# Layer 0's mixing: half of the evictions on ScalarE from 512-column blocks, a quarter of them summed by VectorE

## The chip, the cores and the metric

The kernel runs on one core of a Trainium2 chip. The metric is device time in microseconds (us), median of three runs; less is better. The core has TensorE (PE, matrix products into PSUM), VectorE (DVE), ScalarE (ACT), GpSimd (POOL) and SyncE (SP, here the queue of loads). Each engine works through its own queue in order and waits on semaphores. PSUM has 8 banks; the kernel takes them in four pairs, and calls a pair a bank, and so does this text.

## The reference, cut to what matters

Two graph layers on x of 8 batches, 2048 nodes and 64 channels. In layer 0 every node has its own weights, a mix of 16 shared ones by its embedding:

```python
w = jnp.einsum('nd,dkio->nkio', embedding, weight)      # D = 16, K = 3
b = jnp.einsum('nd,do->no', embedding, bias)
As = [jnp.eye(N), A, 2.0 * (A @ A) - jnp.eye(N)]
x_g = jnp.einsum('knm,bmc->bnkc', jnp.stack(As, 0), x)
out = jnp.einsum('bnki,nkio->bno', x_g, w) + b
x = layernorm(x + out)
```

Layer 1 applies adj twice more and shared weights, adds and normalises again.

## The kernel before

The nodes are 16 tiles of 128. The program has these stages: the first hop (adj times x), the second hop as seven products of half-size blocks, layer 0's mixing (226 to 526 us of the span), the third hop as seven products again, and the last hop with the output.

**Mixing.** For a tile t, `mix0` needs three operands: x, the first hop and the second hop, each transposed and in three parts for precision (`high`, `low`, `mixed`: lines 309 to 322, function `parts`). One product mixes them with the 16 shared weights d, and the 16 results are added up with the node's embedding as factor. Eight batches come as two groups g of four. The work is cut into eight pieces (g, i), each filling one bank `pm`:

- `by_batch` (i = 0 or 1): two batches, d = 0 to 7. 9 pairs of matmuls with 512 columns. ACT evicts it with eight instructions (line 423), each scaled by the embedding, into two SBUF tiles `aside`. When both pieces of a group are there, POOL sums them with three additions (`sum_aside`, line 440) and adds the result to the accumulator `acc` (`add_aside`, line 445).
- `by_four` (i = 4 or 5, and 2 or 3 in place of a `by_batch`): four batches, four d. 18 pairs of matmuls with 256 columns. DVE evicts it with four instructions that multiply by the embedding and add to `acc` (line 433); each of them waits for the one before.

A pair is two matmuls on the two halves of the 128 rows. Before, a tile has two pieces by batch and six by four; the last tile, t = 15, has four of each.

**What stands between the pieces.** The list `at[n]` says what is issued before piece n: the steps of the next tile's operands (`of_x`, `of_hop`, `of_second`), the steps of the previous tile's layernorm (`next(norm)`), `begin_sum` (which starts the next `acc` on POOL), `times_r` (a scaling on POOL for the tile after next), the transposes of the normalised tile (`hT`), and POOL's sums. At a tile's end `project` sends the previous tile's result through layer 1's weights, ACT copies it out (line 475), and the first two steps of x's parts for the tile after next follow. The order of the source is the order of each engine's queue here (`ordered`). In the last tile, `early` starts the operands of the third hop's first steps.

`parts` makes `mixed` in one of two ways: with `quick` by one DVE instruction (line 317), else by an ACT copy and a POOL addition (lines 319 and 320). Before, quick is used for tile 0 alone.

**Buffers.** `hl` tiles come from a pool of HL = 8, `raw` tiles (loads, `aside` and the second hop's parts) from one of RAW = 5. `seven_products` takes four banks for its first product's sums: `sums` is two pairs, and products alternate between them (line 656).

Of the kernel before, what the change touches and what calls it, by code (L numbers as in the profile page):

```python
# [18 lines left out]
P = 128  # L19
# [6 lines left out]
HL = 8  # L26
RAW = 5
# [12 lines left out]
def pattern(  # L40
# [106 lines left out]
    def node_bias(pb):  # L147

        eT, b0_sb = bias_sb[:, : N // 4], bias_sb[:, N // 4 :]
        for j in range(4):  # L150
            for g in range(4):
                q = slice(32 * g, 32 * g + D)
                nc.tensor.matmul(  # L153
                    pb[g // 2][:, g % 2, j * C : (j + 1) * C], lhsT=eT[q, j * P : (j + 1) * P], rhs=b0_sb[q],
                    start=True, stop=True, tile_position=(32 * g, 0),
                )
# [5 lines left out]
    wl = work2.tile([P, 5, C], F32, tag="t0", name="wl")  # L162
    bias_sb = work2.tile([P, N // 4 + C], F32, tag="t0", name="bias_sb")

    loads = [(bias_sb, bias), (pack_sb, pack[:, : NT * D]), (wl.rearrange("p k o -> p (k o)"), pack[:, NT * D + C :])]
# [193 lines left out]
    def layernorm(src):  # L359
# [10 lines left out]
        ordered(nc.vector.tensor_reduce(ss, sq, AX.X, ALU.add))  # L370
        sd, r0, va, q, r = [work.tile([P, B], F32, tag=f"{name}{B}", name=name) for name in ("ln_sd", "ln_r0", "ln_v", "ln_q", "ln_r")]
# [30 lines left out]
    def mix0(t, tt, acc, at, pieces):  # L402
# [14 lines left out]
        def by_batch(g, i):  # L417
            pm = bank("pm").rearrange("p j (d c) -> p j d c", c=C)
            block(pm, 2 * g + i, slice(0, 2 * DG))
            if i == 0:  # L420
                aside[g] = [rawp.tile([P, DG, 2, 2, C], F32, tag="raw", name="aside") for _ in range(2)]
            for d in range(2 * DG):
                ordered(nc.scalar.activation(aside[g][d // DG][:, d % DG, :, i, :], pm[:, :, d, :], AF.Copy, scale=e(d)))  # L423
# [22 lines left out]

        for n, (g, i) in enumerate([*pieces, (None, None)]):
            for work_here in at[n]:
                if isinstance(work_here, tuple):
                    for part in work_here[0]:  # L450
                        {"sum": sum_aside, "add": add_aside}[part](work_here[1])
# [134 lines left out]
    def seven_products(s, to, sums, more, wait=4, raw=()):  # L586
# [31 lines left out]
        def step(p, kk):  # L618
# [38 lines left out]
            def use(got):  # L657
                if p == 0 and kk == 0:
                    sums.extend([bank("accT") for _ in range(2)] for _ in range(2))
# [65 lines left out]
    def operands(t, quick=False):  # L725
# [5 lines left out]
        def begin(k, src):  # L731
# [6 lines left out]
        def of_x():  # L738
            yield from begin(0, xt)

        def of_hop(pt=None):
            yield from begin(1, transposed(z[1][t], pt))

        def of_second():
            yield from begin(2, by_pair(z[2][t]))
# [92 lines left out]
    }, wait=2)  # L838
# [18 lines left out]
    for t in range(NT):  # L857
        got, last = {}, t == NT - 1
        at = [[] for _ in range(9)]
        n1, n2, n3 = [lambda: next(norm)] * 3 if t else [nothing] * 3  # L860

        if not last:
# [3 lines left out]
            at[2] += [go(of_hop), n1, go(of_hop), go(of_hop), n2]  # L866
            if t + 2 < NT:
                at[2] += [lambda: times_r(t + 2)]
                at[4] += [lambda: got.update(coming=operands(t + 2))]
            at[3] += [n3, go(of_second), lambda: got.update(acc=begin_sum(t + 1))]  # L870
            at[4] += [go(of_second), go(of_second)]
            at[6] += [(("sum", "add"), 0)]
            at[7] += [lambda: got.update(hT=transpose(h, "hT"))] if t else []
            pieces = [(0, 0), (0, 4), (0, 5), (1, 2), (0, 1), (1, 3), (1, 4), (1, 5)]
        else:
            at[1] += [n1, n2]
# [5 lines left out]
            at[7] += [(("sum",), 1), lambda: early(2, "y_low"), lambda: early(3, "y_high")]  # L882
            at[8] += [(("add",), 1), lambda: early(3, "y_low")]
            pieces = [(0, 0), (0, 1), (0, 4), (1, 0), (0, 5), (1, 1), (1, 4), (1, 5)]
        norm_now = mix0(t, tt, acc, at, pieces)
# [10 lines left out]
    todo.extend([nothing] * 4 + [lambda: next(norm)] * 3)  # L896
# [479 lines left out]
```

## Time and profile before

| | us |
|---|---|
| median of 3 runs | 764.98 (764.36 to 765.15) |
| profiled execution | 764.04 |
| its span, first to last instruction | 762.3 |
| layer 0's mixing in it | 226.2 to 526.3 |
| a steady tile of the mixing | 18.96 |

In a line of the profile, "out<-in 128x256 x376 | 181.0, 482 | 44.0 <-PE pm L409 32.0" means 376 instructions, 181.0 us busy in union, 482 ns each on average, and 44.0 us in which the engine stood idle just before them, 32.0 of it until PE had finished `pm`. PEld is the weight load of PE. Matmuls overlap, so their length is not their cost; the distance between two starts is.

One tile in the middle, busy us by engine: PE 18.96, DVE 15.26, ACT 10.69, POOL 15.13, of 18.96.

### The profile page before, as it was taken

Reading aid. Unit: us, or ns where it says so; the run is one execution under the profiler, and the core shown is the slowest. Engines: PE = TensorE matmul, PEld = TensorE weight load, DVE = VectorE, ACT = ScalarE, POOL = GpSimd, SP = SyncE. Lnnn points to the kernel's source line nnn. Section 1 sums busy time; section 2 is a strip of 40 time slices with the busy share of each in tenths; the row PEclk is TensorE's granted clock in tenths of the full one; section 3 lists DMA queues with packets and bytes.
Section 4 is the critical chain, followed back from the end, with each engine's and each line's share of the span. In section 5 each row is a group of like instructions: output and inputs, shape, how many; then the busy total and the mean of one; then the engine's idle time right before and its main releaser. Section 6 shows DMA issues by size and latency. Waiting matters only on the chain.

```text
span 762.3 us, 16926 instructions
## 1 busy us (share of the span) xinstructions
PE 753.6 (99%) x6634; PEld 660.6 (87%) x6634; DVE 560.2 (73%) x1159; ACT 406.7 (53%) x896; POOL 269.7 (35%) x297
## 2 busy tenths in 40 slices
PE   9999999999999999999999999999999999999996
PEld 6888888888889999999999999998888888888885
DVE  6768867678757888888888888877688648668663
ACT  5456533877745555555555555558887663112111
POOL 0000000000026877777777777777100000011441
PEclk9999999999999999999999999999999999999999
DMA  8998996555520000000000000003454444565631
GB/s 325 346 393 282 350 312 233 154 177 162 171 69 17 20 20 15 20 18 16 16 16 17 15 16 3 2 16 87 135 167 151 130 154 142 175 177 175 208 127 46
DMA packets 73558, 96.69 MB, mean 127 GB/s; under 512 B 4864, under 2 KB 48384, under 8 KB 73344
## 3 DMA queue, kind: packets, MB, share of 16 engines
q1 hardware_dynamic: 62064, 76.66, 31.8%
q10 hardware_dynamic: 11408, 18.89, 6.6%
q8 instruction: 54, 0.88, 0.5%
q14 instruction: 32, 0.26, 0.1%
HBM read 76.65 MB, written 18.87 MB: 125 GB/s over the span
## 4 chain that ended last, share of the span: by engine, by line
PE 98%; DVE 1%; issue 0%; ACT 0%; DVEq 0%
PE pm L409 36%; PE accT L664 27%; PE acc L254 15%; PE a L254 10%; PE accT L254 6%; PE pu L466 2%; PE pt L300 1%; PE first L143 1%; PE accT L814 1%; DVE acc L433 1%; PE accT L466 0%; PE accT L153 0%; PE accT L300 0%; ACT sq L994 0%; DVE z L289 0%
## 5 line engine op out<-in xcount | busy, mean ns | idle before, releaser
L433 DVE SCALAR_TENSOR_TENSOR acc<-pm,pack_sb,acc 128x256 f32<-128x256 f32 x376 | 181.0, 482 | 44.0 <-PE pm L409 32.0
L409 PE MATMUL pm<-wh,hl 64*128 64x512 f32 (+1 forms) x1332 | 208.0, 303 | 0.0
L664 PE MATMUL accT<-s,hl 128*128 128x512 f32 x896 | 205.9, 390 | 0.8 <-DVE acc L433 0.8
L409 PE MATMUL pm<-wm,parts 64*128 64x512 f32 (+1 forms) x1332 | 203.5, 296 | 0.0
L409 PE MATMUL pm<-wl,parts 64*128 64x512 f32 (+1 forms) x1332 | 203.4, 296 | 0.0
L664 PEld LDWEIGHTS accT<-s,hl 128*128 128x128 f32 x896 | 167.5, 188 | 36.5 <-issue 1.6
L409 PEld LDWEIGHTS pm<-wh,hl 64*128 64x128 f32 x1332 | 130.9, 187 | 4.0 <-issue 0.4
L409 PEld LDWEIGHTS pm<-wl,parts 64*128 64x128 f32 x1332 | 130.8, 187 | 3.7
L409 PEld LDWEIGHTS pm<-wm,parts 64*128 64x128 f32 x1332 | 130.5, 187 | 3.8
L652 ACT CAST s<-raw 128x1024 fp32r<-128x1024 bf16 x104 | 109.9, 1057 | 37.9 <-ACT hl L234 23.4
L254 PE MATMUL acc<-hl,s 128*128 128x512 f32 x512 | 116.8, 390 | 0.0
L254 PEld LDWEIGHTS acc<-hl,s 128*128 128x128 f32 x512 | 96.2, 188 | 20.5 <-issue 0.3
L423 ACT ACTIVATE aside<-pm,pack_sb 128x128 f32<-128x128 f32 x272 | 74.0, 383 | 48.9 <-PE pm L409 48.1
L715 POOL TENSOR_TENSOR z<-z,rrow 128x512 f32<-128x512 f32 x16 | 21.1, 1320 | 212.4 <-DVE z L688 212.4
L234 ACT CAST hl<-z 128x256 fp32r<-128x256 f32 (+1 forms) x96 | 47.7, 515 | 60.1 <-PE acc L254 24.1
L440 POOL TENSOR_TENSOR aside<-aside 128x1024 f32<-128x1024 f32 (+2 forms) x51 | 75.3, 1476 | 4.2 <-ACT aside L423 1.6
L254 PE MATMUL a<-hl,s 128*128 128x512 f32 (+1 forms) x352 | 73.4, 370 | 0.0
L254 PEld LDWEIGHTS a<-hl,s 128*128 128x128 f32 x352 | 61.9, 188 | 11.3
L320 POOL TENSOR_TENSOR parts<-parts 128x512 fp32r<-128x512 f32 x45 | 58.2, 1294 | 35.1 <-DVE parts L314 27.5
L238 DVE TENSOR_TENSOR hl<-z,hl 128x512 fp32r<-128x512 f32 (+1 forms) x96 | 54.7, 577 | 12.9 <-ACT hl L234 10.1
L287 POOL TENSOR_TENSOR z<-z,got 128x512 f32<-128x512 f32 x3 | 4.8, 1631 | 144.4 <-ACT got L286 144.4
L254 PE MATMUL accT<-hl,s 128*128 128x512 f32 x192 | 44.3, 390 | 0.0
(136 smaller groups left out, 814.4 us busy)
## 6 DMA issues: line engine op xcount, KB each, us to landing
raw<-in_adj SPq DMA_DIRECT2D x58, 512.0 KB, 6.1
raw<-sums_of SPq DMA_DIRECT2D x64, 256.0 KB, 2.9
sums_of<-z ACTq DMA_DIRECT2D x16, 512.0 KB, 6.6
raw<-quarters SPq DMA_DIRECT2D x32, 256.0 KB, 2.7
raw<-in_adj SPq DMA_DIRECT2D x16, 384.0 KB, 3.5
quarters<-seen ACTq DMA_DIRECT2D x16, 256.0 KB, 5.8
xt<-in_xT SPq DMA_DIRECT2D x16, 256.0 KB, 2.7
z<-in_x SPq DMA_DIRECT2D x15, 256.0 KB, 6.8
```

Source lines behind the costliest of these rows:

```text
L234: ordered(nc.scalar.copy(to[0], src))
L238: ordered(nc.vector.tensor_tensor(to[1], src, to[0], ALU.subtract))
L254: nc.tensor.matmul(accs[i], lhsT=s[:, i * P : (i + 1) * P], rhs=hl[h], start=(first and h == 0), stop=(last and h == 1),)
L320: ordered(nc.gpsimd.tensor_tensor(mixed, mixed, low, ALU.add))
L409: nc.tensor.matmul(pm[:, j], lhsT=tt[k][n][q, lhsT, :], rhs=w_parts[n][k][q, ds, :], start=(k == 0 and n == 0), stop=(k == 2 and n == 2),)
L423: ordered(nc.scalar.activation(aside[g][d // DG][:, d % DG, :, i, :], pm[:, :, d, :], AF.Copy, scale=e(d)))
L433: ordered(nc.vector.scalar_tensor_tensor(part, got, e(dg * DG + d), part, ALU.mult, ALU.add))
L440: ordered(nc.gpsimd.tensor_tensor(to, to, more, ALU.add))
L466: nc.tensor.matmul(pm[:, j, i * 3 * C : (i + 1) * 3 * C], lhsT=hT[q, 2 * g + i, :], rhs=v[q], start=True, stop=True,)
L652: ordered(nc.scalar.copy(s, got["raw"]))
L664: nc.tensor.matmul(acc[i][:, c], lhsT=hl[h][:, i * P : (i + 1) * P], rhs=S[:, c * 512 : (c + 1) * 512], start=(kk == 0 and h == 0), stop=( ...
L715: ordered(nc.gpsimd.tensor_tensor(to, to, r, ALU.mult))
```

## The change

- In tiles 0 to 14 the pieces are now (1,0), (0,4), (1,1), (0,0), (0,1), (0,5), (1,4), (1,5): four by batch, four by four, and the last three on DVE.
- For group 1 the ACT evictions write into tiles laid out as [2, 64, 8]: d is innermost, so each instruction writes single elements 32 bytes apart, and DVE sums over d with one `tensor_reduce` per piece from contiguous memory (`reduce_aside`) and adds both results to `acc` (`add_reduced`). Group 0 goes by POOL as before.
- `mixed` of x and of the second hop is quick on DVE in all tiles; that of the first hop stays on ACT and POOL.
- Steps between pieces move: hop's transposes, `begin_sum` and `times_r` come before piece 1, the layernorm has one step more (`root` is ACT's square root, apart from the sum before it), and POOL's sum and add are two places.
- In the last tile the low half of the third early operand is issued after the last piece.
- HL is 7 and RAW is 6. The bias is loaded in two parts. The third hop pairs its four sum banks (0, 2) and (1, 3).

```diff
@@ -23,8 +23,8 @@
 DG = 4
 EPS = 1e-5
 FIRST = 8
-HL = 8
-RAW = 5
+HL = 7
+RAW = 6
 WARM = 12
 SLOTS = 3
 SPLIT = 4096.0
@@ -146,7 +146,7 @@
 
     def node_bias(pb):
 
-        eT, b0_sb = bias_sb[:, : N // 4], bias_sb[:, N // 4 :]
+        eT, b0_sb = bias_sb, wl[:, 5]
         for j in range(4):
             for g in range(4):
                 q = slice(32 * g, 32 * g + D)
@@ -159,10 +159,11 @@
         to = ebias[:, 8 * h : 8 * h + 8, :].rearrange("p (g t) c -> p g (t c)", g=2)
         ordered(nc.vector.tensor_copy(to, pb[h][:, :, : 4 * C]))
 
-    wl = work2.tile([P, 5, C], F32, tag="t0", name="wl")
-    bias_sb = work2.tile([P, N // 4 + C], F32, tag="t0", name="bias_sb")
-
-    loads = [(bias_sb, bias), (pack_sb, pack[:, : NT * D]), (wl.rearrange("p k o -> p (k o)"), pack[:, NT * D + C :])]
+    wl = work2.tile([P, 6, C], F32, tag="t0", name="wl")
+    bias_sb = work2.tile([P, N // 4], F32, tag="t0", name="bias_sb")
+
+    loads = [(bias_sb, bias[:, : N // 4]), (wl[:, 5], bias[:, N // 4 :]), (pack_sb, pack[:, : NT * D])]
+    loads += [(wl[:, :5].rearrange("p k o -> p (k o)"), pack[:, NT * D + C :])]
     loads += [(bias1, pack[:, NT * D : NT * D + C]), (rrow, diag.to_broadcast([P, N]))]
 
     def weights():
@@ -368,6 +369,7 @@
         yield
         ss = work.tile([P, B], F32, tag="ln_ss", name="ss")
         ordered(nc.vector.tensor_reduce(ss, sq, AX.X, ALU.add))
+        yield
         sd, r0, va, q, r = [work.tile([P, B], F32, tag=f"{name}{B}", name=name) for name in ("ln_sd", "ln_r0", "ln_v", "ln_q", "ln_r")]
         ordered(nc.scalar.activation(sd, ss, AF.Sqrt, bias=eps, scale=1.0 / C))
         yield
@@ -399,7 +401,7 @@
 
 
 
-    def mix0(t, tt, acc, at, pieces):
+    def mix0(t, tt, acc, at, pieces, on_vector=()):
 
         def block(pm, lhsT, ds):
             for k in range(3):
@@ -417,10 +419,15 @@
         def by_batch(g, i):
             pm = bank("pm").rearrange("p j (d c) -> p j d c", c=C)
             block(pm, 2 * g + i, slice(0, 2 * DG))
-            if i == 0:
-                aside[g] = [rawp.tile([P, DG, 2, 2, C], F32, tag="raw", name="aside") for _ in range(2)]
+            if g in on_vector:
+                aside[g, i] = rawp.tile([P, 2, C, 2 * DG], F32, tag="raw", name="aside")
+                to = [aside[g, i][:, :, :, d] for d in range(2 * DG)]
+            else:
+                if i == 0:
+                    aside[g] = [rawp.tile([P, DG, 2, 2, C], F32, tag="raw", name="aside") for _ in range(2)]
+                to = [aside[g][d // DG][:, d % DG, :, i, :] for d in range(2 * DG)]
             for d in range(2 * DG):
-                ordered(nc.scalar.activation(aside[g][d // DG][:, d % DG, :, i, :], pm[:, :, d, :], AF.Copy, scale=e(d)))
+                ordered(nc.scalar.activation(to[d], pm[:, :, d, :], AF.Copy, scale=e(d)))
 
         def by_four(g, dg):
             dg -= 2
@@ -444,11 +451,21 @@
             one = aside[g][0][:, 0].rearrange("p j i c -> p (j i) c")
             ordered(nc.gpsimd.tensor_tensor(part, part, one, ALU.add))
 
+        def reduce_aside(i):
+            if i == 0:
+                aside["sum"] = xcpool.tile([P, 2, 2, C], F32, tag="ln_xc", name="both")
+            ordered(nc.vector.tensor_reduce(aside["sum"][:, i], aside[1, i], AX.X, ALU.add))
+
+        def add_reduced(_):
+            part = acc[:, 4:8, :].rearrange("p (j i) c -> p i j c", j=2)
+            ordered(nc.vector.tensor_tensor(part, part, aside["sum"], ALU.add))
+
+        does = {"sum": sum_aside, "add": add_aside, "reduce": reduce_aside, "add_reduced": add_reduced}
         for n, (g, i) in enumerate([*pieces, (None, None)]):
             for work_here in at[n]:
                 if isinstance(work_here, tuple):
                     for part in work_here[0]:
-                        {"sum": sum_aside, "add": add_aside}[part](work_here[1])
+                        does[part](work_here[1])
                 else:
                     work_here()
             if n < len(pieces):
@@ -583,7 +600,7 @@
         (S4, "B22", (0, 1)), ((0, 1), "B21", (0, 0)), ((1, 1), "T4", (1, 0)),
     )
 
-    def seven_products(s, to, sums, more, wait=4, raw=()):
+    def seven_products(s, to, sums, more, wait=4, raw=(), pairs=((0, 1), (2, 3))):
 
 
 
@@ -656,7 +673,8 @@
 
             def use(got):
                 if p == 0 and kk == 0:
-                    sums.extend([bank("accT") for _ in range(2)] for _ in range(2))
+                    four = [bank("accT") for _ in range(4)]
+                    sums.extend([four[a], four[b]] for a, b in pairs)
                 acc, hl, S = sums[p % 2], got["hl"], got["s"]
                 for i in range(2):
                     for h in range(2):
@@ -728,7 +746,7 @@
         load(nc.sync, xt, xT[t])
         tt = [None] * 3
 
-        def begin(k, src):
+        def begin(k, src, quick):
             where, tag = ((rawp, "raw"), (spool, "s"))[k != 2]
             high = hpool.tile([P, B // 2, P], F32R, tag="hl", name="hl")
             pair = where.tile([P, 2, B // 2, P], F32R, tag=tag, name="parts")
@@ -736,13 +754,13 @@
             return parts(src, tt[k], by_half if k == 1 else lambda to: to, quick)
 
         def of_x():
-            yield from begin(0, xt)
+            yield from begin(0, xt, True)
 
         def of_hop(pt=None):
-            yield from begin(1, transposed(z[1][t], pt))
+            yield from begin(1, transposed(z[1][t], pt), quick)
 
         def of_second():
-            yield from begin(2, by_pair(z[2][t]))
+            yield from begin(2, by_pair(z[2][t]), True)
 
         return tt, of_x(), of_hop, of_second()
 
@@ -835,7 +853,7 @@
         (0, 6): [last_projected],
         **{(2 + t // KK, t % KK): [lambda t=t: add_bias(t)] for t in range(NT)},
         3: quarter_back(1, 1, 1), 4: quarter_back(0, 1, 0), 5: quarter_back(0, 0, 1),
-    }, wait=2)
+    }, wait=2, pairs=((0, 2), (1, 3)))
 
     third_got = {}
 
@@ -857,32 +875,37 @@
     for t in range(NT):
         got, last = {}, t == NT - 1
         at = [[] for _ in range(9)]
-        n1, n2, n3 = [lambda: next(norm)] * 3 if t else [nothing] * 3
+        n1, n2, root, n3 = [lambda: next(norm)] * 4 if t else [nothing] * 4
 
         if not last:
             following, of_x, of_hop, of_second = coming
             of_hop = of_hop()
             at[1] += [go(of_x)] * (1 if t else 3)
-            at[2] += [go(of_hop), n1, go(of_hop), go(of_hop), n2]
+            at[1] += [n1, lambda: got.update(acc=begin_sum(t + 1))]
             if t + 2 < NT:
-                at[2] += [lambda: times_r(t + 2)]
+                at[1] += [lambda: times_r(t + 2)]
+            at[1] += [go(of_hop)]
+            at[2] += [n2, go(of_hop), go(of_hop), (("reduce",), 0)]
+            at[3] += [root]
+            at[4] += [n3, go(of_second), (("reduce",), 1), (("add_reduced",), 1)]
+            if t + 2 < NT:
                 at[4] += [lambda: got.update(coming=operands(t + 2))]
-            at[3] += [n3, go(of_second), lambda: got.update(acc=begin_sum(t + 1))]
-            at[4] += [go(of_second), go(of_second)]
-            at[6] += [(("sum", "add"), 0)]
+            at[5] += [go(of_second), go(of_second)]
+            at[6] += [(("sum",), 0)]
             at[7] += [lambda: got.update(hT=transpose(h, "hT"))] if t else []
-            pieces = [(0, 0), (0, 4), (0, 5), (1, 2), (0, 1), (1, 3), (1, 4), (1, 5)]
+            at[7] += [(("add",), 0)]
+            pieces, on_vector = [(1, 0), (0, 4), (1, 1), (0, 0), (0, 1), (0, 5), (1, 4), (1, 5)], (1,)
         else:
-            at[1] += [n1, n2]
+            at[1] += [n1, n2, root]
             at[2] += [n3, lambda: early(0, "y_high", *s)]
             at[3] += [(("sum",), 0), lambda: early(0, "y_low")]
             at[4] += [lambda: early(1, "y_high", *s)]
             at[5] += [lambda: early(1, "y_low")]
             at[6] += [(("add",), 0), lambda: got.update(hT=transpose(h, "hT")), lambda: early(2, "y_high")]
-            at[7] += [(("sum",), 1), lambda: early(2, "y_low"), lambda: early(3, "y_high")]
-            at[8] += [(("add",), 1), lambda: early(3, "y_low")]
-            pieces = [(0, 0), (0, 1), (0, 4), (1, 0), (0, 5), (1, 1), (1, 4), (1, 5)]
-        norm_now = mix0(t, tt, acc, at, pieces)
+            at[7] += [(("sum",), 1), lambda: early(3, "y_high")]
+            at[8] += [(("add",), 1), lambda: early(2, "y_low"), lambda: early(3, "y_low")]
+            pieces, on_vector = [(0, 0), (0, 1), (0, 4), (1, 0), (0, 5), (1, 1), (1, 4), (1, 5)], ()
+        norm_now = mix0(t, tt, acc, at, pieces, on_vector)
         if t:
             project(t - 1, got["hT"])
         if "coming" in got:
@@ -893,7 +916,7 @@
         h = next(norm)
         if not last:
             tt, acc = following, got["acc"]
-    todo.extend([nothing] * 4 + [lambda: next(norm)] * 3)
+    todo.extend([nothing] * 4 + [lambda: next(norm), lambda: (next(norm), next(norm)), lambda: next(norm)])
 
 
     def count(name, src):
```

## The prediction

> **What bounds the kernel now.** I read the page first: its engine line, its slices, and the chain of waits by engine.
>
> ```profile
> PE 753.6 (99%) x6634; PEld 660.6 (87%) x6634; DVE 560.2 (73%) x1159; ACT 406.7 (53%) x896; POOL 269.7 (35%) x297
> PE   9999999999999999999999999999999999999996
> ...
> PE 98%; DVE 1%; issue 0%; ACT 0%; DVEq 0%
> PE pm L409 36%; PE accT L664 27%; PE acc L254 15%; PE a L254 10%; PE accT L254 6%; PE pu L466 2%; PE pt L300 1%; PE first L143 1%; PE accT L814 1%; DVE acc L433 1%; PE accT L466 0%; PE accT L153 0%; PE accT L300 0%; ACT sq L994 0%; DVE z L289 0%
> ```
>
> TensorE (PE) is busy in every slice and owns the chain, and the clock was granted at 0.999. "Busy" only means that a matmul is in flight, so next comes the view of waits on PE, which is short:
>
> ```profile
> PE first L143 <- DVE part L144: 1.3, 1, 1.3
> PE accT L664 <- DVE acc L433: 0.8, 1, 0.8
> ```
>
> Columns: total us, times, longest. In the 300 us of layer 0's mixing (L409) PE waits for nobody. So a faster VectorE or ScalarE saves nothing there; fewer or better filled matmuls save time, and so does the one 0.8 us wait. The price of a matmul is the distance between starts, which PE's timeline gives (start, length of the group, count):
>
> ```profile
> 302.39 0.40 PE L409 MATMUL pm<-wm,parts 64*128 64x512 f32 x2
> 302.62 0.29 PE L409 MATMUL pm<-wh,hl 64*128 64x256 f32 x2
> ...
> 304.76 0.41 PE L300 MATMUL pt<-ident,z 64*128 64x64 f32 x8
> ...
> 309.38 0.40 PE L409 MATMUL pm<-wh,hl 64*128 64x512 f32 x2
> ...
> 311.44 0.28 PE L409 MATMUL pm<-wh,hl 64*128 64x256 f32 x2
> ...
> 315.76 0.41 PE L300 MATMUL pt<-ident,xc 64*128 64x64 f32 x8
> ```
>
> A piece of 9 pairs of 512 columns lasts 309.38 to 311.44 = 2.06 us. Two pieces of 18 pairs of 256 last 311.44 to 315.76 = 4.32, so 2.16 each; the one at 302.62 took 2.14. The same columns cost 0.08 to 0.10 us more in blocks of 256: twice as many pairs, each with a small fixed cost. I take 0.09.
>
> The 0.8 us wait stands where layer 0 ends. PE and VectorE (DVE) there:
>
> ```profile
> 526.28 1.47 PE L466 MATMUL pu<-v,hT 64*128 64x192 f32 x16
> 527.69 1.20 PE L664 MATMUL accT<-s,hl 128*128 128x512 f32 x4
> 529.65 0.93 PE L664 MATMUL accT<-s,hl 128*128 128x512 f32 x3 [0.76 <-DVE acc L433]
> ...
> 526.30 1.24 DVE L238 TENSOR_TENSOR hl<-z,hl 128x256 fp32r<-128x256 f32 x1
> 527.47 2.03 DVE L433 SCALAR_TENSOR_TENSOR acc<-pm,pack_sb,acc 128x256 f32<-128x256 f32 x4
> ```
>
> The fifth matmul needs the bank that DVE's last four evictions free. They start at 527.47 because the low half of the third early operand, 1.24 us, stands before them, although their piece was done at 526.28.
>
> Last, a steady tile's busy time by engine, and the prices:
>
> ```profile
> 357.29:376.25 18.96, 18.96 (x289) 18.32 (x287) 15.26 (x32) 10.69 (x33) 15.13 (x18) 1.00 0.06 17
> ...
> L423 ACT ACTIVATE aside<-pm,pack_sb 128x128 f32<-128x128 f32 x272 | 74.0, 383 | 48.9 <-PE pm L409 48.1 <-POOL aside L440 0.8
> L319 ACT ACTIVATE parts<-hl 128x512 fp32r<-128x512 f32 x45 | 29.9, 664 | 0.5
> L314 DVE TENSOR_TENSOR parts<-z,hl 128x512 fp32r<-128x512 f32 x16 | 18.0, 1122 | 6.9 <-ACT hl L312 6.9
> L314 DVE TENSOR_TENSOR parts<-xt,hl 128x512 fp32r<-128x512 f32 x16 | 11.1, 692 | 17.3 <-ACT hl L312 17.3
> ```
>
> The first line is length, PE, PEld, DVE, ACT, POOL. All four others have room under 18.96.
>
> **What the Trainium skill says.** "Advanced Engine Details and Errata", Instruction Support, lists no faster mode for tensor_reduce, so about one element a cycle. The trace agrees: 680 ns for 512 elements (L362), 344 for 192, a slope of 1.05 ns. The same page, GPSIMD Details, says Pool shares an interface with DVE and conflicts with DVE instructions that have two SBUF inputs. The trace agrees: the L314 row from z takes 1.12 us while POOL works, the one from xt 0.69 while POOL mostly idles. "SBUF — State Buffer", Door 1, says each access that crosses to a new 16-byte line pays a penalty, without a size. ScalarE (ACT) will write single 4-byte elements 32 bytes apart; no row of before shows that. "ScalarE: Activation LUTs", What ACT_TABLE_LOAD costs, gives 0.833 ns an element plus fixed costs; L423's 383 ns fit, and its eight follow at 0.25 us.
>
> **The change part by part**, for tiles 0 to 14; tile 15 keeps its pieces.
>
> *PE.* Two pieces of 256 columns become pieces of 512: 15 x 2 x 0.09 = 2.7 us off. Transposes and project stay, so their transitions too. PE's tile: 18.96 - 0.18 = 18.78.
>
> *ACT* gains two pieces, 2 x 2.17 (eight at 0.25, timeline) = 4.34, and loses two mixed copies (L319), 1.33: 10.69 to 13.7. *DVE* loses 8 evictions at 0.52 (4.2), and gains two reductions of 1024 (0.14 + 1024 x 1.05 ns = 1.22 each), an add (0.43, like the 256-element L600), and two mixed parts (0.69, L317 row): 4.25. So DVE isn't relieved: 15.3. *POOL* loses two L320 (1.30 each): 12.5. All hidden while PE waits for no bank and no operand.
>
> That needs a timetable, since queues are in order. Time 0 is a tile's first matmul; the pieces end at 2.21, 4.66 (transposes first), 6.73, 8.79, 10.86, 13.01, 15.18, 17.62 (transposes first), project at 18.78. An eviction starts 0.22 after its piece ends, as in the trace.
> ACT: piece 1, 2.43-4.6. Square at 4.7 (xc comes at 4.68 as before), hop's high half, mixed copy, to 6.7. Piece 3, 6.95-9.1. Root to 9.3. Piece 4 to 11.3. High half of z to 11.8. Piece 5 to 13.8. hT, project copies and the next xt as before (to 1.97 of the next tile).
> DVE: low half of x and the sums, 2.0-3.5; mixed part of x to 4.2 (4.7 beside POOL's xc). Piece 2, 4.9-6.95. ss to 7.5, low half of hop to 8.1, first reduction to 9.3. Reciprocal (waits for the root) to 9.5, second reduction to 10.6, add to 11.0. Low half of z, 11.8-13.0 (priced with POOL's conflict), mixed part to 13.7. Pieces 6, 7, 8 end at 15.7, 17.7 and 19.8.
> Each bank's next user, by the changed program's own assignment, with its slack: piece 4 after piece 1's eviction, 2.1 us; piece 5 after piece 2, 1.8; piece 6 after the hop's low half, 2.7; piece 7 after piece 3, 3.9; piece 8 (15.39) after piece 5, 1.6; the next tile's first piece (18.78) after piece 7, 1.05; its transposes (20.99) after piece 8, 1.2. So no wait; the tightest cover is DVE's 1.05.
>
> The moved sums (begin_sum, times_r) go ahead of hop's mixed part on POOL, 3.2 us of work; that part ends near 9.8 and is read in the next tile. POOL's normalisation ends at 12.4, before the transposes at 15.18. SP keeps its xt load in the same place.
>
> *The handoff.* In tile 15 that 1.24 us low half moves behind the last piece, so its evictions start at 526.28 + 0.2 and end 1.0 us earlier. The first product's second bank is still that piece's, the new pairs notwithstanding. Its wait of 0.8 goes; next late would be the project copies, which end before. 0.8 us off.
>
> *Buffers.* HL 7: the first hop prepares two steps ahead, six tiles; the seventh lets the low half start two steps (2 x 16 x 0.23 = 7.3 us) before use instead of three. PE waits for none of these now; cost 0, at most 1 us. RAW 6 feeds the two new tiles; PE waits for no load, so no gain elsewhere. The split bias load is one more small DMA before 130 us: 0.
>
> Sum: -2.7 - 0.8 = -3.5. The profiled execution took 764.04 (span 762.3 and 1.7 around it), so 760.5; it lies 0.9 below the median of the runs shown (764.98). Against that median: 761.5.
>
> **Rivals.**
> *The handoff wait stays* (the semaphore's delay, or another DVE operation before the evictions): only -2.7, 762.3. The evictions end barely before PE asks, which speaks for it.
> *The gain is handed back as bank waits.* Add, low half of z and mixed part all have two SBUF inputs. If POOL is at work beside each, they cost 0.5 more each (1.19 against 0.69); one is priced in, so DVE's last pieces slip by about 1.0 against 1.05 of slack. A reduction into 128 results instead of 8 might cost more too; 0.1 to 0.3 us more per reduction gives 0.2 us of wait a tile: 15 x 0.2 = 3, 764.5. Against it: POOL has nothing to do from 12.4 to 13.9.
> *Slower: the scattered writes on ACT.* The place is pieces 1 and 3. The fixed part of the 0.25 us is 0.14, the elements' 0.107. Bounds: no penalty, or three times the elements' time (+0.21 each). I take none, since the fixed part dominates. Piece 5 ends later by 16 x the surcharge less the 0.7 us that ACT idles before piece 3; past 1.6 us PE waits. That decides from +0.144 us (pitch 0.39); from 0.165 it is more than the whole gain and 0.2%. At +0.21, 1.1 us a tile: 15 x 1.1 - 3.5 = +13, 778.
>
> **Chances.** Both gains 0.70 (760.6 to 762.4 with 0.08 to 0.10 a piece and the runs' own spread); handoff stays 0.12; handed back 0.09; slower 0.09. A difference of 0.2% (1.5 us) is about what a measurement tells from none. Faster 0.70 + 0.12 = 0.82, the same 0.09, slower 0.09. The range, 760.3 to 763.7, holds the first two and a little of the third.
>
> **What would show it.** Right: tile pitch of 18.78 on PE, no line of waits on PE for L430 or L440, ACT's scattered evictions still 0.25 us apart, reductions of 1.22 us, L664's wait gone. Wrong: PE waiting for ACT's aside before the eighth piece, or for DVE before a tile's first one; reductions near 2 us; pieces of 512 that take more than 2.07 us; waits in the first hop.

## The result, and the profile after

| | before | after |
|---|---|---|
| median of 6 runs, us | 764.67 (764.18 to 765.15) | 760.88 (760.40 to 761.79) |
| ratio, with 95% interval | | 0.9954 [0.9944, 0.9965] |
| profiled execution | 764.04 | 761.79 |
| its span | 762.3 | 759.9 |

The kernel is faster by 0.46%, 3.5 us by the ratio; 3.5 was forecast. None of the six executions took longer than the profiled one, so the stages tell more than the two spans do. First the page of the kernel after: the engines, PE's slices, and the chain of waits by engine and by line.

```profile
PE 750.5 (99%) x6094; PEld 666.6 (88%) x6094; DVE 560.4 (74%) x1114; ACT 455.1 (60%) x1106; POOL 232.9 (31%) x267
PE   9999999999999999999999999999999999999996
...
PE 97%; ACT 1%; POOL 1%; DMA 0%; DVE 0%; issue 0%; POOLq 0%; DVEq 0%
PE pm L411 34%; PE accT L682 27%; PE acc L255 15%; PE a L255 10%; PE accT L255 6%; PE pu L483 3%; PE pt L301 1%; PE first L143 1%; PE accT L832 1%; ACT aside L430 1%; DMA raw<-corner 0%; POOL aside L447 0%; PE accT L483 0%; PE accT L153 0%; ACT s L669 0%
```

PE has 540 matmuls less: 15 tiles x 2 pieces x 9 pairs of two. DVE is as busy as it was (560.2 before); ACT has taken up 48 us, POOL has lost 37. New in the chain, and small, are ACT's aside, POOL's aside and a load, `raw<-corner`: they weren't there before. The view of waits on PE says what they did (total us, times, longest):

```profile
PE first L143 <- DVE part L144: 1.3, 1, 1.3
PE pu L483 <- ACT hT L307: 0.7, 1, 0.7
```

The wait of the third hop's first product on DVE (0.8) is gone, as predicted. In its place stands a wait that the prediction did not have: in tile 15 the project of tile 14's result, the last one in the mixing stage, waits 0.7 us for ACT's copy of the transposed tile.

A steady tile, by the busy view of that stretch (length; then PE, PEld, DVE, ACT and POOL; granted clock, DMA share, GB/s), and PE's timeline in it (start, length of the group, count):

```profile
355.92:374.66 18.74, 18.74 (x253) 18.69 (x251) 15.18 (x29) 13.91 (x47) 12.57 (x16) 1.00 0.05 15
```

```profile
341.83 0.44 PE L411 MATMUL pm<-wh,hl 64*128 64x512 f32 x2
...
343.89 0.44 PE L411 MATMUL pm<-wh,hl 64*128 64x512 f32 x2
...
345.94 0.44 PE L411 MATMUL pm<-wh,hl 64*128 64x512 f32 x2
...
347.98 0.32 PE L411 MATMUL pm<-wh,hl 64*128 64x256 f32 x2
```

The tile takes 18.74 where 18.96 stood, 0.22 less; 0.18 was predicted. The three pieces of 512 columns that now stand in a row (341.83 to 347.98) take 2.06, 2.05 and 2.04 us by these lines; over ten tiles the means are 2.068, 2.040 and 2.040. DVE's 15.18 and POOL's 12.57 are within 0.1 of the predicted 15.3 and 12.5; ACT has 13.91 for 13.7.

The groups of instructions whose prices were open (x count | busy us, mean ns of one | idle before), and ACT's timeline in the same tile:

```profile
L430 ACT ACTIVATE aside<-pm,pack_sb 128x128 f32<-128x128 f32 x512 | 143.9, 484 | 20.3 <-PE pm L411 18.2 <-DVE acc L440 2.1
L457 DVE TENSOR_REDUCE both<-aside 128x128 f32<-128x1024 f32 x30 | 35.6, 1190 | 0.0
L315 DVE TENSOR_TENSOR parts<-z,hl 128x512 fp32r<-128x512 f32 x16 | 12.6, 786 | 18.2 <-ACT hl L313 18.1 <-issue 0.2
```

```profile
358.36 2.31 ACT L430 ACTIVATE aside<-pm,pack_sb 128x128 f32<-128x128 f32 x8 [0.47 <-PE pm L411]
...
362.88 2.33 ACT L430 ACTIVATE aside<-pm,pack_sb 128x128 f32<-128x128 f32 x8 [0.16 <-DVE acc L440]
364.92 0.33 ACT L374 ACTIVATE ln_sd<-ss,eps 128x8 f32<-128x8 f32 x1
365.09 2.22 ACT L430 ACTIVATE aside<-pm,pack_sb 128x128 f32<-128x128 f32 x8
```

The reductions take 1.19 (1.22 predicted). The evictions last longer, 484 ns in the mean of all against 383 before: group 1's, which scatter, last 507 ns, and group 0's, which write as they did, 473. But eight scattered ones still fit into 2.31 us, and the next instruction starts 2.04 after the first (362.88 to 364.92). The distance between starts, the pitch, is 0.255 us, where contiguous ones had 0.252. The low half of z meets POOL less (0.79 in the mean instead of 1.12): it takes 0.69 in nine tiles and 0.91 in seven.

Where the time went, from the starts and ends of PE's matmuls in the two traces:

| us | before | after | gain |
|---|---|---|---|
| steady tile, project to project, x 15 | 18.96 | 18.74 | 3.3 |
| tile 15, project to project | 18.49 | 19.35 | -0.86 |
| last project to the third hop | 1.41 | 1.51 | -0.10 |
| first to fifth matmul of the third hop | 1.96 | 1.03 | 0.93 |
| first matmul of the mixing to the last of the program | 529.44 | 526.18 | 3.26 |

The first row stands for all 15 changed tiles: thirteen gain 0.22 each, and tiles 0 and 1 together 0.43. So the forecast of 3.5 came from 2.7 + 0.8, and the trace has 3.3 and about nothing. Two terms were off, in opposite directions. The experiments are about these two.

### The profile page after: what moved, and what is told of

Read it like the earlier page. It is cut to its first block, busy times and chain, and to the rows that moved or that the text cites. A ratio compares the mean times of both kernels' runs of the same rounds, so it can differ in the third digit from the quotient of the medians.

```text
span 759.9 us, 15977 instructions
## 1 busy us (share of the span) xinstructions
PE 750.5 (99%) x6094; PEld 666.6 (88%) x6094; DVE 560.4 (74%) x1114; ACT 455.1 (60%) x1106; POOL 232.9 (31%) x267
## 4 chain that ended last, share of the span: by engine, by line
PE 97%; ACT 1%; POOL 1%; DMA 0%; DVE 0%; issue 0%; POOLq 0%; DVEq 0%
PE pm L411 34%; PE accT L682 27%; PE acc L255 15%; PE a L255 10%; PE accT L255 6%; PE pu L483 3%; PE pt L301 1%; PE first L143 1%; PE accT L832 1%; ACT aside L430 1%; DMA raw<-corner 0%; POOL aside L447 0%; PE accT L483 0%; PE accT L153 0%; ACT s L669 0%
## 5 line engine op out<-in xcount | busy, mean ns | idle before, releaser
L411 PE MATMUL pm<-wh,hl 64*128 64x256 f32 (+1 forms) x1152 | 214.3, 323 | 0.0
L411 PE MATMUL pm<-wm,parts 64*128 64x256 f32 (+1 forms) x1152 | 209.9, 316 | 0.0
L411 PE MATMUL pm<-wl,parts 64*128 64x256 f32 (+1 forms) x1152 | 209.7, 315 | 0.0
L430 ACT ACTIVATE aside<-pm,pack_sb 128x128 f32<-128x128 f32 x512 | 143.9, 484 | 20.3 <-PE pm L411 18.2
L440 DVE SCALAR_TENSOR_TENSOR acc<-pm,pack_sb,acc 128x256 f32<-128x256 f32 x256 | 123.1, 483 | 27.2 <-PE pm L411 19.7
L411 PEld LDWEIGHTS pm<-wh,hl 64*128 64x128 f32 x1152 | 135.7, 187 | 0.9 <-issue 0.5
L411 PEld LDWEIGHTS pm<-wl,parts 64*128 64x128 f32 x1152 | 135.5, 187 | 0.3
L411 PEld LDWEIGHTS pm<-wm,parts 64*128 64x128 f32 x1152 | 135.2, 186 | 0.4
L669 ACT CAST s<-raw 128x1024 fp32r<-128x1024 bf16 x104 | 109.9, 1057 | 39.5 <-ACT hl L235 28.4
L239 DVE TENSOR_TENSOR hl<-z,hl 128x512 fp32r<-128x512 f32 (+1 forms) x96 | 55.1, 582 | 23.1 <-ACT hl L235 13.7
L492 ACT COPY z<-pu 128x256 f32<-128x256 f32 x90 | 26.3, 400 | 32.1 <-PE pu L483 32.1
```

Of the source, the lines that this page charges most:

```text
L239: ordered(nc.vector.tensor_tensor(to[1], src, to[0], ALU.subtract))
L411: nc.tensor.matmul(pm[:, j], lhsT=tt[k][n][q, lhsT, :], rhs=w_parts[n][k][q, ds, :], start=(k == 0 and n == 0), stop=(k == 2 and n == 2),)
L430: ordered(nc.scalar.activation(to[d], pm[:, :, d, :], AF.Copy, scale=e(d)))
L440: ordered(nc.vector.scalar_tensor_tensor(part, got, e(dg * DG + d), part, ALU.mult, ALU.add))
L492: ordered(nc.scalar.copy(to[k], got[:, :, :, 2 - k, :]))
L669: ordered(nc.scalar.copy(s, got["raw"]))
```

## The experiments

Medians and ratios are against runs of the kernel before on the same chip. "Mixing to end" is the last row of the table above, for which the before has 529.44 and the after 526.18. "First to fifth" is the time from the first to the fifth matmul of the third hop. "Mixing to end" leaves out the first 226 us and the output's tail, which move by up to 2 us and 1.1 us from one profiled execution to the next with the same code in them.

| | median, us | ratio | steady tile | tile 15 | first to fifth | mixing to end |
|---|---|---|---|---|---|---|
| e1_narrow | 763.53 | 0.9986 [0.9979, 0.9992] | 18.93 | 18.79 | 1.04 | 528.52 |
| e9_apart | 761.86 | 0.9968 [0.9957, 0.9978] | 18.76 | 18.78 | 1.03 | 525.97 |
| e5_strided_sum | 763.32 | 0.9988 [0.9979, 0.9996] | 18.74 | 18.86 | 1.03 | 528.09 |
| e6_slow_mixed | 761.04 | 0.9954 [0.9941, 0.9968] | 18.74 | 19.48 | 1.03 | 526.24 |
| e7_hl6 | 761.85 | 0.9965 [0.9952, 0.9977] | 18.74 | 18.95 | 1.03 | 525.78 |
| e2_late_cast | 760.57 | 0.9943 [0.9930, 0.9956] | 18.74 | 18.49 | 1.04 | 525.20 |
| e11_after | 761.98 | 0.9958 [0.9945, 0.9972] | 18.74 | 19.38 | 1.03 | 526.24 |
| e12_late_cast | 760.33 | 0.9940 [0.9927, 0.9954] | 18.74 | 18.49 | 1.04 | 525.19 |
| e3_late_cast_low_first | 760.71 | 0.9943 [0.9931, 0.9955] | 18.74 | 18.49 | 1.24 | 525.48 |
| e4_low_first | 762.62 | 0.9969 [0.9958, 0.9980] | 18.74 | 18.81 | 2.78 | 527.40 |
| e10_before_low_last | 762.79 | 0.9973 [0.9962, 0.9984] | 18.96 | 18.49 | 1.04 | 528.50 |

### What the width of the blocks is worth

**e1_narrow**: the kernel after, with group 1's two pieces mixed in blocks of 256 columns, so that everything but PE's block size is as after.

```diff
-            block(pm, 2 * g + i, slice(0, 2 * DG))
+            if g in on_vector:
+                for half in range(2):
+                    ds = slice(half * DG, (half + 1) * DG)
+                    block(pm[:, :, ds], 2 * g + i, ds)
+            else:
+                block(pm, 2 * g + i, slice(0, 2 * DG))
```

> The changed kernel, but group 1's two by-batch pieces of tiles 0 to 14 as 18 pairs of 256 columns; evictions, order and buffers stay. Theory A (only PE's own pitch counts; everything else is hidden): the steady tile goes from 18.74 back to about 18.96, so 15 x 0.22 = 3.3 us are lost and some 0.5 us of gain against the kernel before remain, ratio near 0.999. Rival B (the gain comes from evictions moved off VectorE): the time stays near 761, ratio near 0.995.

The busy view of a steady tile of e1 (as above):

```profile
356.42:375.35 18.93, 18.93 (x288) 18.44 (x287) 15.13 (x28) 13.90 (x45) 12.63 (x16) 1.00 0.06 16
```

DVE, ACT and POOL have what they have after, and the tile is back at 18.93. So 18.93 - 18.74 = 0.19 of the 0.22 is the width alone, 0.094 in the mean of the two pieces; the prediction had 0.09. The two are not alike: from PE's starts, the first piece of a tile accounts for 0.066, and the third, which in the kernel after stands ahead of two more pieces of 512, for 0.121. By the ratios 0.0032 of the gain is gone, 2.45 us (0.9986 against 0.9954), of 15 x 0.187 = 2.8 in the trace. With e1's remaining ratio of 0.9986, what isn't width is 1.1 us.

The other 0.033 of each tile (18.960 to 18.927) is what e1 keeps. It has as many blocks of each width as the kernel before, in another order. PE's starts show what the order does: a piece of 512 columns takes 2.068 us behind a piece of 256, in both kernels and in e1, and 2.040 behind another piece of 512, in the kernel after and in e1; the kernel before has no such neighbours.

**e9_apart**: the pieces in another order, so that the three blocks of 512 do not stand in a row.

```diff
-            pieces, on_vector = [(1, 0), (0, 4), (1, 1), (0, 0), (0, 1), (0, 5), (1, 4), (1, 5)], (1,)
+            pieces, on_vector = [(1, 0), (0, 4), (1, 1), (1, 4), (0, 0), (0, 1), (0, 5), (1, 5)], (1,)
```

> The changed kernel with the pieces in the order (1,0), (0,4), (1,1), (1,4), (0,0), (0,1), (0,5), (1,5): VectorE's pieces two last instead of three, one more change between blocks of 512 and of 256 per tile. Theory A: PE's pitch grows by 0.02 to 0.03 us a tile, 0.4 us in all; VectorE does piece (1,4) before its reductions and nothing waits: ratio 0.9955 to 0.9965. Rival H (three last is needed): the reductions come 2 us later, the layernorm's end and the operands with them, and PE waits for the normalised tile or a bank, 0.3 us a tile or more: 765 or more.

A tile takes 18.76, 0.02 more, without any wait on PE in a steady tile. One more piece of 512 now stands behind a piece of 256 and takes 2.068 instead of 2.040; a piece of 256 gives 0.008 of that back. So the order has a price of its own. From mixing to end the run is not slower than after (525.97), since its tile 15 came out 0.57 shorter, for a reason shown below. Its median is 1 us higher, with overlapping intervals; the profile is of the fastest of its eight executions (761.36), and no stretch of the mixing shows why the others took longer.

### Whether the layout of the sums matters

**e5_strided_sum**: ACT writes contiguous rows, and DVE reads its eight terms 512 bytes apart.

```diff
-                aside[g, i] = rawp.tile([P, 2, C, 2 * DG], F32, tag="raw", name="aside")
-                to = [aside[g, i][:, :, :, d] for d in range(2 * DG)]
+                aside[g, i] = rawp.tile([P, 2 * DG, 2, C], F32, tag="raw", name="aside")
+                to = [aside[g, i][:, d] for d in range(2 * DG)]
...
-            ordered(nc.vector.tensor_reduce(aside["sum"][:, i], aside[1, i], AX.X, ALU.add))
+            ordered(nc.vector.tensor_reduce(aside["sum"][:, i], aside[1, i].rearrange("p d j c -> p j c d"), AX.X, ALU.add))
```

> The changed kernel, but for group 1 ScalarE writes runs of 64 elements with d outermost, and VectorE's reduction reads single elements 512 bytes apart. Theory A (scattered writes cost ScalarE no rate, and the layout matters only if VectorE's slack of about 1 us is used up): if the strided reduction takes 1.2 us as the contiguous one, the time is that of the changed kernel, ratio 0.9954. Rival E (the contiguous layout is what makes the change pay): the reduction takes 1.7 us or more, VectorE's last pieces come over 1 us later, PE waits a few tenths a tile, and the time is 764 or more.

Its groups of ACT's evictions and of DVE's reductions:

```profile
L430 ACT ACTIVATE aside<-pm,pack_sb 128x128 f32<-128x128 f32 x512 | 141.4, 426 | 20.3 <-PE pm L411 18.2 <-DVE acc L440 2.1
...
L457 DVE TENSOR_REDUCE both<-aside 128x128 f32<-128x1024 f32 x30 | 59.8, 1995 | 0.0
```

The same sums cost 1.995 us instead of 1.19. ACT's 512 evictions are 58 ns shorter in the mean; 240 of them are the ones that no longer scatter, so 512 x 58 / 240 = 124 ns each. Taken apart, group 1's last 384 ns here and 507 after, and group 0's last 473 in both, so why those are longer than the 383 of the kernel before stays open. The pitch of group 1's is 0.252 us here and 0.255 after, and the busy time in union falls by only 2.5 us in the whole program. The scattering costs latency, and next to nothing in pitch. Now DVE is late, which the view of waits on PE and DVE's timeline in tile 0 show:

```profile
PE pm L411 <- DVE acc L440: 1.4, 1, 1.4
...
PE pm L411 <- ACT aside L430: 0.6, 1, 0.6
```

```profile
235.52 3.93 DVE L457 TENSOR_REDUCE both<-aside 128x128 f32<-128x1024 f32 x2
...
240.86 2.77 DVE L318 SCALAR_TENSOR_TENSOR parts<-hl,parts 128x512 fp32r<-128x512 f32 x1
243.56 6.13 DVE L440 SCALAR_TENSOR_TENSOR acc<-pm,pack_sb,acc 128x256 f32<-128x256 f32 x12
```

Each wait occurs once, in tile 1; steady tiles still take 18.74. In tile 0 the longer sums push a mixed part to 240.86, onto POOL's additions (from 240.31), and it takes 2.77 us instead of 0.69; in the kernel after it starts at 239.12, ahead of POOL's additions (240.11). The lateness is passed on: tile 1's project comes 2.4 us later after the mixing's start than in the kernel after, less what the wait in tile 15 shrinks, 1.9 to the end. The contiguous layout is thus worth 1.9 us in the trace (0.0034 by the ratio, 2.6 us), not by its steady price but because tile 0 has no room for the slow sums. Rival two of the prediction, a gain handed back as bank waits, has this mechanism; the kernel after stays short of it.

### The parts that were priced at nothing

**e6_slow_mixed**: `mixed` of x and of the second hop again on ACT and POOL.

```diff
-            yield from begin(0, xt, True)
+            yield from begin(0, xt, quick)
...
-            yield from begin(2, by_pair(z[2][t]), True)
+            yield from begin(2, by_pair(z[2][t]), quick)
```

> The changed kernel with the mixed parts of x and of the second hop back on ScalarE and POOL. Theory A: ScalarE has room (about 14.4 of 18.74 us busy, 15.7 then) and POOL too (15.1), so no wait of PE but perhaps a few tenths in all; ratio 0.995 to 0.996. Rival F (ScalarE's queue is at its limit): its fifth piece ends after 15.4 us of the tile, PE waits for it, over 0.3 us a tile, 765 or more.

Ratio 0.9954, as after; tile 18.74. Its steady tile has POOL 15.32 and DVE 14.23 busy (after 12.57 and 15.18), and PE still waits for neither in the tile. Priced rightly at 0.

**e7_hl6**: one `hl` buffer less still.

```diff
-HL = 7
+HL = 6
```

> The changed kernel with HL 6 instead of 7. Theory A: seven leave a spare step in every stage, so even six cost little: at most a wait of some tenths in each of the first hop's 30 steps if low halves come late, time between 761 and 762. Rival G (HL is tight, so going from 8 to 7 has already cost something): six cost 2 us or more, with waits of PE for ScalarE's or VectorE's hl in the hops.

From mixing to end it takes 525.78, no more than after. Its mixing begins 1.3 us later, at 227.64. Of this, 0.76 lies in the second hop, which takes 104.31 us from its first matmul to the mixing; in each of the other twelve traces, those of both kernels among them, it takes 103.55. PE waits for no `hl` there. In the kernel after, the node bias's 32 small products run in one block; in e7 they run as 4 and 28, with eight matmuls of the hop between them. The ratio agrees (0.0011 above after, 0.8 us), though the intervals overlap. So one buffer less still seems to cost 0.8 us, by another way than either theory had it. The step from 8 to 7 was not run alone. But the first hop takes 116.4 us before and 116.5 after, and the second 103.55 in both, so that step shows no cost.

The new pairs of sum banks and the split bias load were not run alone either. From the third hop's fifth matmul to the last matmul of the program PE takes 226.0 us in both kernels, so neither shows a cost.

### The handoff: which wait is left, and whose it is

In tile 15 the chain of waits of the kernel after runs as follows (start, us, what):

```profile
514.51 2.61 POOL aside L447
...
517.14 3.19 DMA raw<-corner
...
520.35 1.05 ACT s L669
521.39 2.07 ACT aside L430 x8
523.47 0.48 ACT hT L307
...
523.99 1.57 PE pu L483 x16
```

A load for the third hop's second early operand starts when POOL's first addition of group 0 ends (517.14), and lands 3.19 us later. ACT's cast of it (L669, called by `early(1, "y_high")`) stands in ACT's queue ahead of the last group of evictions and of the copy to `hT`; these wait behind it, and PE waits for the copy. In the kernel before the same part of ACT's timeline, whose lines have other numbers, reads:

```profile
521.67 1.05 ACT L652 CAST s<-raw 128x1024 fp32r<-128x1024 bf16 x1
522.62 2.17 ACT L423 ACTIVATE aside<-pm,pack_sb 128x128 f32<-128x128 f32 x8
524.63 0.64 ACT L306 COPY hT<-pt 128x512 f32<-128x512 f32 x1
```

Here the cast waits for no load (no bracket), and the copy ends at 525.27, 1.0 us ahead of the project at 526.28; in the kernel after it ends at 523.95, and the project starts 0.04 later.

What differs is when the load may start, and so which buffer it gets. Before, it starts at 518.47, when ACT's cast of the first early load has ended (518.44), so it takes that load's buffer; it lands at 521.65, just in time for its own cast. After, it starts when POOL's first addition ends, and what this addition reads for the last time is the second of group 0's two `aside` tiles: that is the buffer it takes. Counted from the project before it, the load starts 12.49 us into tile 15 instead of 10.67. No run separates whether the sixth buffer or the new `aside` tiles that draw on the pool changed the buffer.

How much is lost depends on how long the load takes. In the eight traces that keep the cast in its place, the load starts 12.45 to 12.58 us after that project. Where it takes 2.65 to 2.80 us (e1, e9, e5, e7, e4), tile 15 takes 18.78 to 18.95; where it takes 3.19 to 3.26 (after, e11, e6), 19.35 to 19.48.

**e2_late_cast**: the load stays where it is issued; the cast moves behind the transposes' copy in ACT's queue.

```diff
-            at[4] += [lambda: early(1, "y_high", *s)]
+            at[4] += [lambda: early(1, "y_high", "load_sum")]
...
-            at[7] += [(("sum",), 1), lambda: early(3, "y_high")]
+            at[7] += [(("sum",), 1), lambda: early(1, "operands"), lambda: early(3, "y_high")]
```

> The changed kernel; in tile 15 ScalarE's cast of the second early load is issued after hT's copy instead of before the last by-batch eviction. Theory A: the new 0.7 us wait of project on hT in tile 15 comes from that cast, which waits for a load whose buffer POOL frees late; it goes, VectorE's evictions still end in time, and 0.7 us more are gained: 760.2, ratio 0.9945. Rival C: hT is late for another reason or PE then waits for VectorE's last evictions instead; no gain, 760.9.

ACT's timeline of e2 in tile 15, and PE's:

```profile
518.94 2.17 ACT L430 ACTIVATE aside<-pm,pack_sb 128x128 f32<-128x128 f32 x8 [1.07 <-PE pm L411]
520.95 0.64 ACT L307 COPY hT<-pt 128x512 f32<-128x512 f32 x1
521.41 0.47 ACT L235 CAST hl<-z 128x256 fp32r<-128x256 f32 x1
521.72 1.12 ACT L669 CAST s<-raw 128x1024 fp32r<-128x1024 bf16 x1
```

```profile
523.32 1.50 PE L483 MATMUL pu<-v,hT 64*128 64x192 f32 x16
524.75 5.57 PE L682 MATMUL accT<-s,hl 128*128 128x512 f32 x23
```

The evictions now wait for PE alone, the copy is done 1.7 us before the project, and tile 15 takes 18.49 as it did in the kernel before. From mixing to end 0.98 us are gained.

**e11_after and e12_late_cast**: the kernel after and e2 once more, side by side.

> The changed kernel once more, beside the next run on the same chip: ratio 0.9954, about 760.9, with one wait of 0.7 us on ACT's copy to hT in tile 15. There is no rival here; it is the reference for the next run.

> The changed kernel with the second early operand's cast behind the copies of the projected tile, once more. Theory A (the cast that waits for its late load holds up ACT's copy to hT): 0.7 to 0.85 us below the run of the changed kernel beside it, ratio about 0.9944. Rival B (what the earlier run gained was the scatter of runs): the same as that run within 0.3 us.

The trace gives 1.05 us between the two (526.24 and 525.19), the medians 1.65, the ratios 0.0018, which is 1.4 us. The first pair had 0.0011, 0.84 us. So the wait is worth about 1 us in these two pairs of traces; where the load lands sooner, tile 15 loses only 0.3 against its 18.49. This version, at 0.9943 and 0.9940, is clearly faster than the kernel before, and below the kernel after in both pairs, though the intervals of each pair still overlap.

**e10_before_low_last**: the kernel before with only the low half moved behind the last piece.

```diff
-            at[7] += [(("sum",), 1), lambda: early(2, "y_low"), lambda: early(3, "y_high")]
-            at[8] += [(("add",), 1), lambda: early(3, "y_low")]
+            at[7] += [(("sum",), 1), lambda: early(3, "y_high")]
+            at[8] += [(("add",), 1), lambda: early(2, "y_low"), lambda: early(3, "y_low")]
```

> The kernel before with the third early operand's low half alone moved behind VectorE's last piece of tile 15; no width or layout is changed. Theory A (the wait of the third hop's first product on VectorE, 0.8 us, is a cost of its own in the kernel before, where the load that comes late in tile 15 of the changed kernel isn't late): the wait goes, no wait on the project copies comes, ratio 0.9989, about 763.9. Rival B (something else then ends last there, so that the move alone is worth nothing): ratio 1.000, and another wait of about 0.8 us in tile 15 or at the start of the third hop.

PE's timeline of e10 at the handoff; before, a second row of L664 began 1.96 us after the first with a wait on DVE:

```profile
526.40 1.47 PE L466 MATMUL pu<-v,hT 64*128 64x192 f32 x16
527.80 4.46 PE L664 MATMUL accT<-s,hl 128*128 128x512 f32 x18
```

The first 18 matmuls run through, and mixing to end is 0.94 shorter: the move by itself is worth what the prediction said (0.8), and that nothing is left of it in the kernel after is the doing of the late load, not of the move. The kernel before has little room here, too: e10's load took 3.83 us, ACT's cast waited 0.62 for it, and the copy to `hT` ended 0.36 ahead of the project. The timed ratio, 0.9973 [0.9962, 0.9984], says 1.2 to 2.9 us, which is more than this trace shows; the rest is open.

**e4_low_first**: the kernel after with the low half back ahead of the last piece.

```diff
-            at[7] += [(("sum",), 1), lambda: early(3, "y_high")]
-            at[8] += [(("add",), 1), lambda: early(2, "y_low"), lambda: early(3, "y_low")]
+            at[7] += [(("sum",), 1), lambda: early(2, "y_low"), lambda: early(3, "y_high")]
+            at[8] += [(("add",), 1), lambda: early(3, "y_low")]
```

> The changed kernel with that low half before the last piece again and the cast where the change has it. Theory A (the two waits cover each other: while project waits for hT, VectorE has time): no wait of the first product or one of 0.2 at most, the same time as the changed kernel, 760.9 to 761.1. Rival D (the moved low half gave 0.8 as the prediction had it): 0.8 slower, 761.7.

Waits on PE in e4, and DVE's timeline:

```profile
PE accT L682 <- DVE acc L440: 1.6, 1, 1.6
```

```profile
524.10 1.90 DVE L239 TENSOR_TENSOR hl<-z,hl 128x256 fp32r<-128x256 f32 x1 [0.48 <-ACT hl L235]
525.93 2.03 DVE L440 SCALAR_TENSOR_TENSOR acc<-pm,pack_sb,acc 128x256 f32<-128x256 f32 x4
```

The two waits do not cover each other; the one on DVE comes back, and with 1.6 us it is twice what it was. The low half needs ACT's high half, which the late cast delays too, and then takes 1.90 us while POOL adds. The evictions begin at 525.93, after the third hop's first matmul (525.32). So in the kernel after the move keeps away 1.2 us (527.40 against 526.18; 0.0015, 1.15 us, by the ratios), more than its price in the kernel before. In these two traces e4's load also landed 0.54 sooner; first to fifth alone differs by 1.75.

**e3_late_cast_low_first**: both edits of e2 and e4.

```diff
-            at[4] += [lambda: early(1, "y_high", *s)]
+            at[4] += [lambda: early(1, "y_high", "load_sum")]
...
-            at[7] += [(("sum",), 1), lambda: early(3, "y_high")]
-            at[8] += [(("add",), 1), lambda: early(2, "y_low"), lambda: early(3, "y_low")]
+            at[7] += [(("sum",), 1), lambda: early(1, "operands"), lambda: early(2, "y_low"), lambda: early(3, "y_high")]
+            at[8] += [(("add",), 1), lambda: early(3, "y_low")]
```

> As e2, with the low half of the third early operand issued before the last piece again, as before the change. Theory A: the 0.8 us wait of the third hop's first product on VectorE comes back, 0.8 slower than e2, so near 761.0. Rival: the order of that low half is worth nothing, same as e2.

DVE's timeline of e3:

```profile
524.58 0.53 DVE L239 TENSOR_TENSOR hl<-z,hl 128x256 fp32r<-128x256 f32 x1
525.04 2.03 DVE L440 SCALAR_TENSOR_TENSOR acc<-pm,pack_sb,acc 128x256 f32<-128x256 f32 x4
```

The expected 0.8 us did not come back: first to fifth is 1.24 instead of 1.04. With ACT's high half on time the low half takes 0.53 us, not the 1.24 it took in the kernel before, and the evictions begin early enough. So the place of the low half costs 0.2 to 0.3 us here (525.48 against e2's 525.20 from mixing to end), and more where a late input or POOL makes it slow.

## Why the prediction was right, and where it was not

**PE's blocks: right in mechanism, too small.** The term was 15 x 2 x 0.09 = 2.7. The tile lost 0.22, not 0.18, so 3.3. Two pieces of 256 columns that took 2.144 and 2.160 gave way to two of 512 that took 2.040 each, so a piece was worth 0.11. The prediction took its 2.06 from a piece of 512 behind one of 256 and used it for every piece inside the tile (2.06 and 2.07 in its timetable). "Transposes and project stay, so their transitions too" looks at those alone, and not at two pieces of 512 in a row. That e1's mean of 0.094 comes so close to 0.09 is partly chance, since its two pieces gave 0.066 and 0.121.

**No wait in the steady tiles: right.** PE waits for no bank and no operand in them. The open prices came out at the values that were taken: ACT's pitch stays at 0.25 us, reductions took 1.19 for 1.22, DVE 15.2 for 15.3. e5 shows how close the limit was: 0.8 us more in each reduction and the collision in tile 0 costs 1.9 us.

**The slower rival: excluded.** It needed a surcharge on ACT's pitch of 0.144 us. The scattered writes lengthen an instruction by 0.12, but eight in a row start 0.255 us apart instead of 0.252, so almost nothing of it reaches the pitch.

**The handoff: the step that failed.** "Its wait of 0.8 goes; next late would be the project copies, which end before. 0.8 us off." The wait on DVE went (0.93 between first and fifth matmul), but the next late was in front of it: ACT's copy to `hT`, 0.86 in tile 15 and 0.10 at its project. Net nothing. The cause is in the sentence on buffers, "PE waits for no load, so no gain elsewhere": six `raw` buffers were examined for what they feed, not for which buffer each later load then inherits. The second early load of tile 15, whose cast stands in ACT's queue, fell to a buffer that POOL frees late. e2 and e12 show the size, e10 that without it the 0.8 was right. The size is partly chance: the same late start costs 0.3 to 1.0 us in tile 15, by how long the load takes.

**Buffers and quick copies at nothing: right** for the quick copies (e6) and, as far as the hops of both kernels show, for HL 7. One less still lengthens the second hop by 0.76 (e7). For the sixth `raw` buffer and the new `aside` tiles together it was wrong, as just said.

So the sum, 3.5, agrees with 3.3 + 0 by the trace and 3.5 [2.7, 4.3] by the runs, though one term lacked 0.6 and another had 0.8 too much. That the total was met so closely is luck. The forecast's 761.5 is 0.6 above the 760.88 measured, half of it because the kernel before itself came out at 764.67 and not 764.98. The likeliest case, both gains together, happened in its sum and not in its parts.

## What to carry to other kernels

When a pool changes its size or gains a user, look again at the buffer of every later request, and for a load ask who last read the buffer that it inherits: an instruction that waits for a load holds up everything behind it in its queue, here a copy that had 0.4 to 1.0 us to spare. Where a bound engine waits for nobody, count its own work precisely, and measure a block's price beside the neighbours that it will have. And test a sum term by term: here its total hid two errors that each were a fifth of it.

## What the runs showed of the hardware

- ACT's instructions that write 4-byte elements 32 bytes apart last 0.12 us longer (507 ns after, 384 in e5), and the time between starts hardly changes (0.255 and 0.252 us). "SBUF — State Buffer", Door 1, in the Trainium skill speaks of a penalty for accesses that cross to a new 16-byte line; for these writes the runs show little more than a longer latency.
- DVE's reduction of 1024 elements to 128 takes 1.19 us from contiguous memory and 1.995 where the eight terms of a sum lie 512 bytes apart (after and e5). Two in a row take 3.93 us in e5, so here the time is lost in full.
- A mixing piece of 512 columns takes PE 2.068 us behind a piece of 256 columns and 2.040 behind another of 512 (after, e9).
- What a DVE instruction with two SBUF inputs loses beside POOL varies much: 0.69 us alone, 2.77 in e5's tile 0 beside POOL's addition of 1024 elements; for 256 columns, 0.42 alone and 1.90 in e4.
